# Folding the value and output weights, and moving the heads to partition quarters, in a Mamba and local-attention kernel

## The chip, the cores and the metric

The kernel runs on one core of one Trainium2 chip. The metric is device time in microseconds of one execution. The kernel before was run three times, and it has one profiled execution besides, taken by the hardware profiler. All times below are microseconds unless marked ns.

A core has five engines which run in parallel, each working through its own instructions in order: TensorE (PE, matrix products; its weight loads are shown apart as PEld), VectorE (DVE), ScalarE (ACT), GpSimd (POOL) and SyncE (SP). Here SyncE issues all DMA transfers of the kernel. Engines wait for each other through semaphores only.

## The reference, cut to what matters

The input x has 4 sequences of 1024 tokens with 128 features. First x gets a residual block: a layer norm, another, and two Mamba blocks (forward and backward scan over 1024 steps with 256 channels and 16 states). Then come six layers, each of them local attention and a feed-forward part, both with a residual:

```python
def attn_layer(x, Wqkv, qs, ksc, Wo):        # x: shifted tokens, 16 heads of 64
    q, k, v = split heads of (x @ Wqkv)
    q = l2norm(q) * qs;  k = l2norm(k) * ksc
    q = q * cos * scale + rotate_half(q) * sin * scale
    k = k * cos / scale + rotate_half(k) * sin / scale
    out = local_attention(q, k, v)            # windows of 32, each sees itself and the one before
    return out.reshape(b, n, INNER) @ Wo

def ffn_layer(x, g, bln, W1, b1, W2, b2):
    xn = (x - mu) / sqrt(var + 1e-05) * g + bln
    a, gate = split(xn @ W1 + b1, 2)          # 341 each
    return a * gelu(gate) @ W2 + b2
```

In local_attention the scores of a window of 32 queries against 64 keys are multiplied by 8, masked, put through a softmax, and multiplied with v. All is f32.

What the change rests on: for one head, attn @ (x Wv) @ Wo equals attn @ (x (Wv Wo)), since the product of a head's 128x64 value weights with its 64x128 output weights can be made ahead.

## The kernel before

The program has three parts. **Prepare** (class Prepare, L131 to L552) goes through eight units (four sequences, two directions): layer norms, input projections, convolution, the step sizes of the scan; what the scan needs is written to DRAM. On six of the units it also prepares one layer each: rotary tables times the q and k scales (lr, rm, rs), and the feed-forward weights scaled by the layer norm's gain (lf loads, fp and fv fold the bias, fa scales, fs stores). **Beside** (class Beside) does the scan: 512 steps of 128 rows (8 channels by 16 states) by 512 tokens, with one exponential on ScalarE (`decay`, L699), a product (`input`, L706 to L714), the scan on VectorE (`scan`, L731), a product on GpSimd (`output`, L744) and, for four steps, four column-quarter matmuls (`add`, L766). The first 134 steps lie in Prepare, the rest beside the layers. **Layers** (class Layers) does the six layers on tiles of 256 tokens, 96 tiles in all (four sequences, six layers, four tiles).

The order of the instructions is written out by hand in tables. ORDER has one entry for each operation with the number of tiles by which it lags: the row is run once a tile, so operations of five tiles are mixed. In ORDER six steps of Beside stand in each row (xd, xi, xr, xo, xt); once the scan is over, LAST_ORDER is used, which has none. FIRST_ORDER does the same for Prepare. All engines take their instructions in the order in which the tables issue them. Matmul results go to five PSUM banks that are handed out in turn (`one`).

One tile of Layers, operation by operation:

- `q` (L969 to L978): tokens are 128 rows, 512 columns of q or k weights are streamed; eight matmuls 128x512. `sq` (L981) squares on ScalarE, `rr` and `ro` (L994) multiply with the rotary tables on VectorE, `n` (L1002) sums squares, `ra` (L1007) adds the rotated halves on GpSimd, eight of 128x512, `nr` makes the inverse norms, `rs` (L1020) applies them.
- `v` (L1026) makes the values, four matmuls 128x512; `va` (L1032) copies them out; `vs` (L1042, L1043) makes a copy shifted by 32 rows by DMA, so that a window and the one before lie in one set of 64 rows.
- `t` and `qk` (L1057, L1067) transpose q and k on TensorE. `s`, `z` (L1078, L1096) write the mask and 128 small products into PSUM: query rows of a window in a quarter of the partitions (window number), head pairs and window halves along the columns. `mx`, `e`, `ex`, `sm`, `ew` (L1106 to L1127) are the softmax: maximum, subtraction (VectorE), one exponential of 128x1024 for eight heads (ScalarE), sum and reciprocal (VectorE), product (GpSimd).
- `te`, `at` (L1134, L1140) transpose the weights on TensorE and copy them out; `w`, `y` (L1159) multiply them with v, 128 matmuls of 64x64 by 32; `oe` (L1170) copies out, `pw` (L1181) multiplies with the output weights, eight matmuls of 128x256.
- `xf` to `xs` (L1199 to L1288): residual, norm, feed-forward part. `ge` adds the bias, `gelu` takes the table for Gelu in and the other back after it.

The weights of a layer are loaded for each sequence anew. `weight` counts the uses, and after the last one puts the next load on a list, `later`; the row's loop then issues one of the list at a time, on SP. Fetches of the scan's rows (`steps`, L671) go through SP as well.

## Time and profile before

| | |
|---|---|
| median of three runs | 4055.16 |
| lowest, highest | 4049.41, 4068.73 |
| span of the profiled execution | 4070.2 |
| mean granted TensorE clock | 0.959 |
| instructions | 145466 |
| HBM read, written | 381.42 MB, 51.67 MB |

The page shows nothing of the profiled execution outside its span, so the span stands for its own time; it is 15 us above the median of the runs.

How to read it: busy times are sums over one engine; a share near 100% says that the engine has hardly any idle time, not that each of its instructions is as short as it could be, since matmuls are pipelined and their ends are modelled. The groups' busy sums of TensorE overlap with one another, so what a group costs is better read from the chain of waits, or from the distance between starts in the timeline. The digits in the page's slices are tenths of a slice, of 101.8 us each.

### The profile page before, as it was taken

Reading aid. Unit: us, or ns where it says so; the run is one execution under the profiler, and the core shown is the slowest. Engines: PE = TensorE matmul, PEld = TensorE weight load, DVE = VectorE, ACT = ScalarE, POOL = GpSimd, SP = SyncE. Lnnn points to the kernel's source line nnn. Section 1 sums busy time; section 2 is a strip of 40 time slices with the busy share of each in tenths; the row PEclk is TensorE's granted clock in tenths of the full one; section 3 lists DMA queues with packets and bytes.
Section 4 is the critical chain, followed back from the end, with each engine's and each line's share of the span. In section 5 each row is a group of like instructions: output and inputs, shape, how many; then the busy total and the mean of one; then the engine's idle time right before and its main releaser. Section 6 shows DMA issues by size and latency. Waiting matters only on the chain.

```text
span 4070.2 us, 145466 instructions
## 1 busy us (share of the span) xinstructions
PE 3825.5 (94%) x62248; PEld 2447.0 (60%) x62248; DVE 3397.9 (83%) x5081; ACT 2975.5 (73%) x5581; POOL 3164.3 (78%) x2589
## 2 busy tenths in 40 slices
PE   5899859999999999999999999999999999999998
PEld 1333226666666666666666666666666666666665
DVE  3677769999899999999999999999777777777774
ACT  4577737887777787787777887877667777677775
POOL 2767669999889898998998998988666666566662
PEclk6788869999999999999999999999999999999999
DMA  5688855555545555555555555554221222122211
GB/s 156 190 268 267 250 178 149 148 161 154 149 133 159 145 154 153 161 151 148 154 145 142 156 156 158 153 151 118 58 65 54 64 58 74 52 63 57 66 50 40
DMA packets 319415, 540.05 MB, mean 133 GB/s; under 512 B 41795, under 2 KB 123467, under 8 KB 318771
## 3 DMA queue, kind: packets, MB, share of 16 engines
q1 hardware_dynamic: 318770, 530.75, 45.5%
q8 instruction: 492, 8.06, 0.9%
q14 instruction: 153, 1.25, 0.1%
HBM read 381.42 MB, written 51.67 MB: 106 GB/s over the span
## 4 chain that ended last, share of the span: by engine, by line
PE 70%; ACT 12%; DVE 7%; POOL 6%; issue 4%; DMA 1%; SPq 1%; DVEq 0%; ACTq 0%; POOLq 0%
PE pq L974 12%; PE po L1159 10%; PE pw L1181 8%; PE pv L1026 7%; PE pt L1057 6%; PE sim L1096 5%; PE pe L1134 4%; PE pm L290 3%; PE py L1278 3%; PE pa L1262 3%; PE pg L1238 2%; ACT sq L981 2%; PE acc L766 2%; DVE sh L731 1%; PE sim L1078 1%
## 5 line engine op out<-in xcount | busy, mean ns | idle before, releaser
L1007 POOL TENSOR_TENSOR r<-r,rot 128x512 f32<-128x512 f32 x768 | 964.1, 1274 | 83.2 <-DVE rot L994 71.1
L1020 POOL TENSOR_TENSOR r<-r,n 128x1024 f32<-128x1024 f32 x384 | 726.2, 1905 | 261.3 <-ACT n L1016 253.2
L974 PE MATMUL pq<-w,xsa 128*128 128x512 f32 x1536 | 799.0, 615 | 2.7 <-ACT at L1140 1.6
L744 POOL TENSOR_TENSOR sh<-sh,sc 128x512 f32<-128x512 f32 x512 | 649.9, 1274 | 96.9 <-DVE sh L731 66.7
L981 ACT ACTIVATE sq<-pq 128x512 f32<-128x512 f32 x768 | 448.2, 599 | 254.0 <-PE pq L974 125.4
L994 DVE TENSOR_TENSOR rot<-pq,tab 128x512 f32<-128x512 f32 x768 | 516.4, 683 | 133.9 <-ACT sq L981 111.0
L994 DVE TENSOR_TENSOR r<-pq,tab 128x512 f32<-128x512 f32 x768 | 518.1, 683 | 82.1 <-PE pq L974 40.3
L1127 POOL TENSOR_TENSOR e<-e,sm 128x1024 f32<-128x1024 f32 x192 | 365.5, 1904 | 243.6 <-DVE sm L1123 228.4
L1057 PEld LDWEIGHTS pt<-ident,r 128*128 128x128 f32 x3072 | 359.1, 142 | 242.5 <-issue 119.1
L1057 PE MATMUL pt<-ident,r 128*128 128x128 f32 x3072 | 443.4, 277 | 37.0 <-POOL r L1020 15.2
L1002 DVE TENSOR_REDUCE n<-sq 128x16 f32<-128x1024 f32 x384 | 456.6, 1210 | 0.0
L1159 PEld LDWEIGHTS po<-at,vs 64*64 64x64 f32 x12288 | 332.3, 135 | 198.3 <-issue 153.8
L1159 PE MATMUL po<-at,vs 64*64 64x32 f32 x12288 | 400.0, 223 | 21.5 <-issue 12.3
L1159 PE MATMUL po<-at,v 64*64 64x32 f32 x12288 | 391.6, 220 | 5.9 <-issue 5.8
L1026 PE MATMUL pv<-w,xsa 128*128 128x512 f32 x768 | 383.4, 601 | 0.2 <-ACT qT L1067 0.2
L1181 PE MATMUL pw<-o,wos 128*128 128x256 f32 x1536 | 377.9, 389 | 1.7 <-ACT o L1170 1.7
L731 DVE TENSOR_TENSOR_SCAN sh<-da,carry,sh 128x512 f32<-128x512 f32 x256 | 327.1, 1278 | 43.7 <-ACT da L699 41.2
L731 DVE TENSOR_TENSOR_SCAN sh<-da,sh 128x512 f32<-128x512 f32 x256 | 311.5, 1217 | 57.2 <-ACT da L699 50.6
L1096 PEld LDWEIGHTS sim<-kT,qT 64*32 64x32 f32 x24576 | 264.5, 106 | 141.8 <-issue 134.7
L1159 PEld LDWEIGHTS po<-at,v 64*64 64x64 f32 x12288 | 334.6, 136 | 9.0 <-issue 8.9
L699 ACT ACTIVATE da<-sdt,b_nega 128x512 f32<-128x512 f32 x378 | 260.5, 689 | 108.2 <-DVE sh L731 92.7
L974 PEld LDWEIGHTS pq<-w,xsa 128*128 128x128 f32 x1536 | 257.0, 191 | 125.8 <-issue 49.0
(160 smaller groups left out, 7598.5 us busy)
## 6 DMA issues: line engine op xcount, KB each, us to landing
sdt<-dts SPq DMA_DIRECT2D x756, 256.0 KB
vs<-v SPq DMA_DIRECT2D x192, 384.0 KB
fdt<-dts SPq DMA_DIRECT2D x204, 256.0 KB
w<-in_wqkv SPq DMA_DIRECT2D x288, 128.0 KB
tab<-tabs SPq DMA_DIRECT2D x96, 256.0 KB
vs<-v SPq DMA_DIRECT2D x168, 128.0 KB
wos<-in_wo SPq DMA_DIRECT2D x96, 128.0 KB
dts<-e SPq DMA_DIRECT2D x32, 256.0 KB
```

Source lines behind the costliest of these rows:

```text
L731: self.nc.vector.tensor_tensor_scan(h, self.da.pop(n), h, self.carry[:, at : at + 1] if t else 0.0, ALU.mult, ALU.add)
L744: self.nc.gpsimd.tensor_tensor(h, h, self.unit[k][2], ALU.mult)
L974: self.nc.tensor.matmul(pq, lhsT=self.tokens(t, i), rhs=w[:, g * 512 : (g + 1) * 512], start=True, stop=True)
L981: self.nc.scalar.activation(sq[:, g * 8 : g * 8 + 8], pq, AF.Square)
L994: self.nc.vector.tensor_tensor(out[:, g * 8 : g * 8 + 8], pq, tab, ALU.mult)
L1007: self.nc.gpsimd.tensor_tensor(r[:, :, to], r[:, :, to], rot[:, :, of], ALU.add)
L1020: self.nc.gpsimd.tensor_tensor(r, r, bc(n2[:, a, :], 2, [P, H, DH]), ALU.mult)
L1026: self.nc.tensor.matmul(pv, lhsT=self.tokens(t, i), rhs=w[:, g * 512 : (g + 1) * 512], start=True, stop=True)
L1057: self.nc.tensor.transpose(pt[:, j * P : (j + 1) * P], rf[:, (g * 4 + j) * P : (g * 4 + j + 1) * P], self.c["ident"],)
L1096: self.nc.tensor.matmul(t.bank["s", g, par][r * W : (r + 1) * W, col : col + 64], lhsT=qT[rows, g * 4 + j, at : at + W], rhs=kT[rows, g * ...
L1159: self.nc.tensor.matmul(t.bank["w", g, x][64 * par : 64 * par + 64, j * P + r * W : j * P + (r + 1) * W], lhsT=v[rows, col : col + DH], rh ...
L1181: self.nc.tensor.matmul(t.bank["pw"], lhsT=wos[:, g * 4 + h, :], rhs=t.tiles["o", g][:, h, :], start=(g == 0 and h == 0), stop=(g == 1 and ...
```

## The change

**The values.** Prepare gets operations that load a layer's value and output weights (wl), multiply them head by head (wp, 16 matmuls of a 64x128 by 64x128 pair), copy the products out (we) and store them (ws) as `wvo`, 16 matrices of 128x128. In Layers `v` now makes, for each window of 32 tokens, x Wv Wo of all heads: the heads are in four groups, and a group's results lie in a quarter of the partitions. `te`, `at`, `vs`, `y` and `pw` go.

**The heads on quarters.** `s` and `z` put head pair c of a half in quarter c of the partitions, and windows along the columns. The 32x32 blocks of the softmax weights are then transposed in place by VectorE (`tp`), and `w` sums over heads inside the matmul (128 rows are four heads by 32 keys): 64 matmuls of 128x32 by 128 a tile. `oe` copies 128x256, `ot` transposes it back.

**The softmax.** For one half of the heads (SINGLE) the maximum is negated, and the exponential is taken straight from PSUM, one of 64 columns for each head and window with the maximum as bias and the sum as a second output (`ea`), then `rc`; `e`, `ex`, `sm` stay for the other half.

**Smaller.** q's and k's columns are ordered so that a matmul holds one half of all heads; `rr`, `ro` and `sq` write with a stride, and `ra` becomes one addition of 128x1024 for each of four. The feed-forward weights are centred in Prepare (fc, fe), so `xn` reads xf and `xnc` goes. `ge` goes into `gelu` as a bias. `pg` and `pa` put two products in one bank. Weight loads stand in the tables (lw, lwv, l, ll, lt), with two buffers for wvo and lv and one for the others. xdbl and w1s in Prepare have one buffer instead of two. `decay`, `scan` and `output` get conditions on the others' progress. FIRST_ORDER, ORDER and LAST_ORDER are new.

The core of the diff, without the tables:

```diff
+    def fc(self, u, g):
+        if u.l is not None:
+            pm = u.bank["fc", g] = self.one("pm")[:, 0:FI]
+            self.nc.tensor.matmul(
+                pm, lhsT=self.c["center"], rhs=u.tiles["w1s", 0][:, g * FI : (g + 1) * FI],
+                start=True, stop=True,
+            )
+
+    def fe(self, u, g):
+        if u.l is not None:
+            self.nc.scalar.copy(
+                u.tiles["w1s", 0][:, g * FI : (g + 1) * FI], u.bank["fc", g]
+            )
...
+    def wl(self, u):
+        if u.l is not None:
+            for k, name in enumerate(("wvl", "wol")):
+                w = u.tile(self.sp, name, 0, [P, NHP, D])
+                self.nc.sync.dma_start(out=w, in_=self.values[k][u.l])
+
+    def wp(self, u, g, par):
+
+        if u.l is not None:
+            pm = u.bank["wp", g, par] = self.one("pm")
+            rows = slice(64 * par, 64 * par + 64)
+            for k in range(4):
+                self.nc.tensor.matmul(
+                    pm[:, k * D : (k + 1) * D], lhsT=u.tiles["wvl", 0][rows, g * 4 + k, :],
+                    rhs=u.tiles["wol", 0][rows, g * 4 + k, :], start=True, stop=True,
+                )
+
+    def we(self, u, g, par):
+        if u.l is not None:
+            self.nc.scalar.copy(
+                u.tiles["wol" if par else "wvl", 0][:, g * 4 : g * 4 + 4],
+                u.bank["wp", g, par].rearrange("p (k m) -> p k m", m=D),
+            )
+
+    def ws(self, u, par):
+        if u.l is not None:
+            of = u.tiles["wol" if par else "wvl", 0]
+            for g in range(2):
+                self.nc.sync.dma_start(
+                    out=self.values[2][u.l, :, :, 2 * g + par, :], in_=of[:, g * 4 : g * 4 + 4]
+                )
...
+    def load(self, name, l, *of):
+        tile_ = partial(self.wp.tile, dtype=F32, name=name, bufs=1 + (name in TWICE))
+        if name[:2] == "qk":
+            w = tile_([P, 512])
+            at = int(name[2]) * H * DH + int(name[3]) * 512
+            pairs = [(w, wqkv[l, :, at : at + 512])]
+        elif name == "wvo":
+            w = tile_([P, 4, 4 * D])
+                (w[:, c].rearrange("p (n m) -> p n m", m=D), wvo[l, :, c]) for c in range(4)
...
+    def begin(self, t, name):
+        if t.sb == 0 and t.k:
+            self.load(name, t.l)
+
+    def lw(self, t, a, g):
+        self.begin(t, f"qk{a}{g}")
...
-    def ra(self, t, i, a, x):
-        r, rot = t.tiles["r", (i, a)], t.tiles["rot", (i, a)]
-        to, of = slice(x * W, x * W + W), slice(W - x * W, 2 * W - x * W)
-        self.nc.gpsimd.tensor_tensor(r[:, :, to], r[:, :, to], rot[:, :, of], ALU.add)
+        self.nc.vector.tensor_reduce(
+            n2[:, a, :], t.tiles["sq", (i, a)].rearrange("p h x e -> p h (x e)"), AX.X, ALU.add
+        )
+
+    def ra(self, t, i, a):
+        r = t.tiles["r", (i, a)].rearrange("p h x e -> p (h x e)")
+        rot = t.tiles["rot", (i, a)].rearrange("p h x e -> p (h x e)")
...
-    def v(self, t, i, g):
-
-        w = self.weight("w2", t)
-        pv = t.bank["v", i, g] = self.one("pv")
-        self.nc.tensor.matmul(
-            pv, lhsT=self.tokens(t, i), rhs=w[:, g * 512 : (g + 1) * 512], start=True, stop=True
-        )
-
-    def va(self, t, i, g):
-        v = t.tile(self.sp, "v", i, [P, H * DH], 4)
-        self.nc.scalar.copy(v[:, g * 512 : (g + 1) * 512], t.bank["v", i, g])
-
-    def vs(self, t, i):
-
-        nc, v = self.nc, t.tiles["v", i]
-        vs = t.tile(self.sp, "vs", i, [P, H * DH], 4)
-        if t.sb == 0 and i == 0:
-            nc.gpsimd.memset(vs[0:W], 0.0)
-        else:
-            before = t.tiles["v", 0] if i else self.tile_at(t, -1).tiles["v", 1]
-            nc.sync.dma_start(out=vs[0:W], in_=before[P - W : P])
-        nc.sync.dma_start(out=vs[W:P], in_=v[0 : P - W])
+    def v(self, t, w):
+
+        wvo = self.weight("wvo", t)
+        pv = t.bank["v", w] = self.one("pv")
+        at = W + t.sb * SB + w * W
+        for c in range(4):
+            self.nc.tensor.matmul(
+                pv[c * W : (c + 1) * W], lhsT=self.xsa[t.b % 2][:, at : at + W], rhs=wvo[:, c],
+                start=True, stop=True,
+            )
+
+    def va(self, t, w):
+        vw = t.tile(self.sp, "vw", w, [P, 4, D], VALUES)
+        self.nc.scalar.copy(vw, t.bank["v", w].rearrange("p (n m) -> p n m", m=D))
...
+    def products(self, t, g, windows):
         qT, kT = t.tiles["qT", 0], self.kT
-        for j in js:
-            for x in range(2):
-                for r in range(4):
-                    at = P * (r // 2) + 64 * x + W * (r % 2)
-                    for par in range(2):
-                        rows = slice(64 * par, 64 * par + 64)
-                        col = (j * 2 + x) * 64
-                        self.nc.tensor.matmul(
-                            t.bank["s", g, par][r * W : (r + 1) * W, col : col + 64],
-                            lhsT=qT[rows, g * 4 + j, at : at + W],
-                            rhs=kT[rows, g * 4 + j, at : at + 2 * W],
-                            start=False, stop=(j == 3 and x == 1),
-                        )
+        for w in windows:
+            for c in range(4):
+                for par in range(2):
+                    rows = slice(64 * par, 64 * par + 64)
+                    self.nc.tensor.matmul(
+                        t.bank["s", g, par][c * W : (c + 1) * W, w * 64 : (w + 1) * 64],
+                        lhsT=qT[rows, g * 4 + c, w * W : (w + 1) * W],
+                        rhs=kT[rows, g * 4 + c, w * W : (w + 2) * W],
+                        start=False, stop=(w == 7),
+                    )
...
+        self.nc.vector.tensor_reduce(
+            mx[:, par * 8 : par * 8 + 8], sv, AX.X, ALU.max, negate=g in SINGLE
+        )
+
+    def ea(self, t, g, par):
+
+        e = t.tile(self.sp, "e", g, [P, 16, 2 * W], 2)
+        sm = t.tile(self.sp, "sm", g, [P, 16], 2)
+        mx = t.tiles["mx", g]
+        sv = t.bank["s", g, par].rearrange("p (n j) -> p n j", j=2 * W)
+        for w in range(8):
+            n = par * 8 + w
+            self.nc.scalar.activation(
+                e[:, n], sv[:, w], AF.Exp, bias=mx[:, n : n + 1], accum_out=sm[:, n : n + 1]
+            )
+
+    def rc(self, t, g):
+        sm = t.tiles["sm", g]
+        self.nc.vector.reciprocal(sm, sm)
...
-    def te(self, t, g, par):
-
-        ef = t.tiles["e", g].rearrange("p (h x) j -> p h (x j)", x=2)
-        pe = t.bank["te", g, par] = self.one("pe")
-        for j in range(4):
...
+    def tp(self, t, g):
+
+        eT = t.tile(self.sp, "eT", g, [P, 2, 8, 2, W], 2)
+        self.nc.vector.transpose(
+            eT.rearrange("p a w x q -> p (a w x q)"),
+            t.tiles["e", g].rearrange("p n j -> p (n j)"),
+        )
+
+    def w(self, t, g, i):
+
+        if g == 0 and i == 0:
+            t.bank["o"] = self.one("po")[:, 0:SB]
+        t.weighted += 1
+        eT = t.tiles["eT", g]
+        before = None if t.sb == 0 else self.tile_at(t, -1)
+        begun = set()
+        for par in range(2):
+            for x in range(2):
+                for r in range(4):
+                    at = 4 * i + r - 1 + x
+                    of = t if at >= 0 else before
+                    if of is None:
+                        continue
+                    first = g == 0 and i == 0 and r not in begun
+                    begun.add(r)
+                    self.nc.tensor.matmul(
+                        t.bank["o"][r * W : (r + 1) * W, i * D : (i + 1) * D],
+                        lhsT=eT[:, par, 4 * i + r, x, :],
+                        rhs=of.tiles["vw", at % 8][:, 2 * g + par, :],
+                        start=first, stop=(t.weighted == 4 and par == 1 and x == 1),
+                    )
+
+    def oe(self, t):
+        self.nc.scalar.copy(t.tile(self.sp, "o", 0, [P, SB], 2), t.bank["o"])
+
+    def ot(self, t):
+
+        pw = t.bank["pw"] = self.one("pw")[:, 0:SB]
+        for i in range(2):
             self.nc.tensor.transpose(
...
-    def pw(self, t, g):
...
-    def xnc(self, t):
-        self.nc.scalar.copy(t.tile(self.sp, "xn", 0, [P, SB]), t.bank["pd"])
...
     def xn(self, t):
-        xn = t.tiles["xn", 0]
-        self.nc.vector.tensor_tensor(xn, t.bank["pvar"], xn, ALU.mult)
+        self.nc.vector.tensor_tensor(
+            t.tile(self.sp, "xn", 0, [P, SB]), t.bank["pvar"], t.tiles["xf", 0][:, 0:SB], ALU.mult
+        )
...
     def scan(self):
+        if self.at["scan"] == min(self.at["decay"], self.at["input"]):
+            return
...
+SINGLE = (1,)
...
+TWICE = "wvo", "lv"
```

Of the new tables, the part of ORDER that holds `w` and what follows it:

```text
ro100-1 rr100-1 sq100-1 xo-0 xr-0 s1-2 ra10-1 z1-2 rr111-1 l1-3 sq111-1 lw11-0 v6-3 mx10-2 xt-0
w00-3 lw10-0 xq-0 va6-3 xa-0 rs00-1 w01-3 ro111-1 xd-0 lt-0 mx11-2 w10-3 xo-0 w11-3 lw00-0 xi-0
xp-0 py0-4 sm0-2 ea10-2 xp-0 n10-1 oe-3 py1-4 ot-3 xq-0 xq-0 py2-4 v2-2 n11-1 t001-1 ea11-2 ll-3
xf-3 ew0-2 xo-0 va2-2 nr1-1 xi-0 t000-1 xs-4 xr-0 qk001-1 t011-1 qk000-1 t010-1 xq-0 q011-0
qk010-1 qk011-1 sq011-0 rs10-1 rc1-2 tp0-2 xp-0 lw01-0 q001-0 pd-3 xd-0 xt-0 rr011-0 xq-0 xt-0
```

## The prediction

> **What bounds the kernel now.** I read the page first, then the busy time of the engines in two stretches, then the chain of waits of the second stretch, then stretches of the timeline. The page's span is 4070.2 us. TensorE is nearly full from slice 6 on; VectorE and GpSimd are nearly full only in slices 6 to 27.
>
> ```profile
> span 4070.2 us, 145466 instructions
> PE 3825.5 (94%) x62248; PEld 2447.0 (60%) x62248; DVE 3397.9 (83%) x5081; ACT 2975.5 (73%) x5581; POOL 3164.3 (78%) x2589
> PE   5899859999999999999999999999999999999998
> DVE  3677769999899999999999999999777777777774
> POOL 2767669999889898998998998988666666566662
> PEclk6788869999999999999999999999999999999999
> ```
>
> So there are three stages: *prepare* (0 to about 600 us), the *main loop* (600 to about 2830, Layers and Beside together, table ORDER) and the *last loop* (to the end, Layers alone, LAST_ORDER). Next come the two loops by engine. The columns are the stretch, its length, busy time of PE, PEld, DVE, ACT and POOL, clock, DMA share and GB/s.
>
> ```profile
> 700.00:2800.00 2100.00, 2041.20 (x36450) 1366.84 (x36450) 1975.32 (x2873) 1628.52 (x3105) 1917.30 (x1574) 1.00 0.54 151
> 2900.00:3900.00 1000.00, 983.08 (x18179) 680.98 (x18178) 756.25 (x1171) 725.16 (x1396) 630.57 (x448) 1.00 0.21 60
> ```
>
> VectorE's subtractions `e` (four a tile, below) number 227 and 116 there, so the stretches hold 56.75 and 29.0 tiles. One tile takes 37.0 us in the main loop (PE 36.0, DVE 34.8, POOL 33.8, ACT 28.7) and 34.5 us in the last (PE 33.9, DVE 26.1, ACT 25.0, POOL 21.7). TensorE bounds both, at 97 and 98%; in the main loop VectorE stands 6% behind it. From 600 to 2830 there are 60 tiles' time, from 2830 to 4070 36.
>
> The chain of waits for 2900 to 3900 us shares that time out by line, free of the overlap that the groups' busy sums contain:
>
> ```profile
> by line: PE pq L974 21.1%; PE po L1159 12.5%; PE pw L1181 11.1%; PE pv L1026 10.4%; PE pt L1057 9.8%; PE sim L1096 8.5%; PE pe L1134 5.4%; PE pg L1238 4.1%; PE py L1278 3.8%; PE pa L1262 3.7%; PE sim L1078 2.4%; PE pd L1207 1.3%; PE pvar L1
> ```
>
> Of 34.5 us a tile: po 4.31, pw 3.83, pv 3.59, pe 1.86.
>
> **The change, TensorE.** These four go: -13.6 us a tile. In their place come 32 matmuls of 128x512 in column quarters for v, 64 of 128x128 in quarters for w, and 2 transposes. Nothing in the old layers has that form, but Beside's add does: four quarters of 128x512, each in two passes. The timeline (start, length, engine, line, what, count; a start minus the one before is what the step really costs):
>
> ```profile
> 1511.05 1.06 PE L766 MATMUL acc<-sh,wide 128*32 128x512 f32 x8
> 1512.05 0.66 PE L1057 MATMUL pt<-ident,r 128*128 128x128 f32 x4
> ...
> 3318.66 1.02 PE L974 MATMUL pq<-w,xsa 128*128 128x512 f32 x2
> 3319.52 1.02 PE L1026 MATMUL pv<-w,xsa 128*128 128x512 f32 x2
> 3320.37 1.02 PE L974 MATMUL pq<-w,xsa 128*128 128x512 f32 x2
> ...
> 3330.80 1.13 PE L974 MATMUL pq<-w,xsa 128*128 128x512 f32 x2
> 3331.86 0.32 PE L1159 MATMUL po<-at,vs 64*64 64x32 f32 x8
> ```
>
> Four quarters take 1.00 us, one full matmul 0.86; so quarters do run side by side. A full one between two other array shapes takes 1.06: a change of shape costs about 0.1. For v, 8 windows give 6.9 us without any change of shape and 8.0 at the add's price; the tables put v in about five groups, so 6.9 + 5 x 0.14 = 7.6. For w, 16 groups of four quarters, each a quarter of the 512 columns, 0.215 us: 3.4, with entries 3.7. The upper end for w is that its 128 weight loads don't hide: L1159's loads show 332.3 us for 12288, 27 ns each, +3.5 us; I take the low end since add's loads (128x32 as well) hide. The transposes cost 2 x 0.11 (four `pt` in 0.44). Sum +11.5: net **-2.0 us a tile** (-3.0 to +1.5). TensorE: 31.9 in the last loop, 34.0 in the main loop.
>
> **VectorE.** Out: two subtracts `e` (0.60 each from start to start) and one sum `sm` (1.21); in: two 32x32 transposes of 128x1024. The rotary products, `n`, `mx` keep their sizes, only with runs of 32 elements; `xn` too. No transpose is in the trace. Its nearest rows are passes over the same 1024 elements:
>
> ```profile
> L1112 DVE TENSOR_TENSOR e<-sim,mx 128x512 f32<-128x512 f32 x227 | 145.5, 684 | 0.0
> L1122 DVE TENSOR_REDUCE sm<-e 128x16 f32<-128x1024 f32 x114 | 138.2, 1212 | 1.8
> ```
>
> From 1.21 (one pass) to 2.42 (two) each; I take 1.21, as every f32 row of 1024 on VectorE stands near it. Sum -2.4 + 2.4: VectorE stays at 34.8 and 26.1. The Trainium skill (VectorE: DVE Perf Modes, The three transpose paths) gives 311 ns for a 128x128 bf16 transpose; as an estimate, eight of these are 2.49 us, which is the bad end, and no run here shows one yet.
>
> **ScalarE.** `at` (4) goes and `va` doubles (+4): equal. `oe` 4x512 becomes 1x256: -1.7. One `ex` of 1024: -0.97. `xnc` -0.28, `ge` 3 x 0.40 = -1.2, gelu three instead of two +0.3. In come 16 exponentials of 64 elements with a bias column and a running sum. The nearest row, `n` 128x32 with a bias column, has 0.32; 32 more elements at (0.597 - 0.372)/256 us make 0.35. Back-to-back copies overlap by 0.1 (two in 1.07 against 0.587 each), so 0.25 is the low end; no overlap and one more instruction for the sum, priced at the shortest row (0.188, L1194), is the high end, 0.54. I take 0.375: +6.0 (4.0 to 8.6). Net +2.2: 27.2 and 30.9 us, at worst 29.8 and 33.5, still under TensorE and VectorE. The rule that speaks against this part is in the Trainium skill (ScalarE: Activation LUTs, What ACT_TABLE_LOAD costs): about 280 ns fixed with a bias column plus 0.833 ns an element, an estimate of 333 ns here and 5.3 us for 16; by it ScalarE would be 0.7 us lower.
>
> **GpSimd.** `ra` 8 x 1.274 (L1007) becomes 4 of 1024 elements; the row with two full inputs (x1b, L245) has 2.354: -0.8, so 33.0 and 20.9. Not a bound.
>
> **SyncE and DMA.** The 360 shifted copies of v go, with SP's waits ahead of them (225 us in the main loop, 773 in the last, at L1043). The weights' bytes for a layer are the same 2 MB plus FFN. A load now stands at a fixed place behind its last reader; it waits at SP's head, and fetches of sdt are queued behind it. The reader of qk01 is issued some 70 entries ahead of the load, so I price this at nothing; if the cover fails, one 256 KB load late by about 3 us on every fourth tile is 24 x 3 = 72 us.
>
> **Prepare.** Six units gain 16 matmuls of 64x128 by 128 (4 x 0.215 x 4 = 3.4 us on TensorE), two of 128x341 (1.1), six copies on ScalarE (4 x 0.5 + 2 x 0.45 = 2.9), and 2 MB of DMA (wl, ws), 12 MB against 131 MB up to 600 us. From 200 to 500 us PE is 91% busy at clock 0.83 and DMA 84%. w1s, wvl and wol have one buffer, so each next load waits on SP until the store has landed, with the fetches of dt behind it; they run five steps ahead. 4.5/0.83 x 6 = 33 us if TensorE's part shows in full; below, nothing; above, with DMA (12 MB at 260 GB/s = 46 us) some 70. I take **+30**.
>
> **Sum.** Last loop: 31.9/0.983 = 32.5, -2.0 x 36 = -72 us. Main loop: VectorE, 34.8, is late next, with TensorE 34.0 and GpSimd 33.0 close behind. VectorE's idle there is 6%, most of it released by PE; at 97% a tile takes 35.9, -1.1 x 60 = -66. The new conditions on decay, scan and output let all six steps of a row pass except two outputs of the first, so the scan ends at most one row later (35.9 - 32.5 = 3 us, within the rounding). Prepare +30. Together -108: 3962 for the profiled execution. Its span is 15 us over the median of the runs (4055.2; nothing outside the span is shown), so **3947** on the median, -2.7%.
>
> **Rivals.**
> - *More*: v at 6.9 with few shape changes, VectorE at 98.5% in the main loop, prepare hidden: -3.0 x 36 - 1.65 x 60 = -207, 3848. For it: the new tables have 11 and 13 shape changes in TensorE's order where the old had 14 and 18. Against: four engines within a few per cent seldom leave only 1.5% idle.
> - *Main loop gains nothing*: 37.0 stays, since VectorE, GpSimd, five PSUM banks and ScalarE's queue (eight exponentials in a row hold two banks and keep `sq` and `qk` behind them) give back what TensorE is spared; prepare +50: -72 + 50 = -22, 4033.
> - *Slower*: the transpose takes two passes, 2.42. Main loop: VectorE 34.8 + 2.4 = 37.2, at 97% 38.4, +84 us; the last loop keeps its -72 (VectorE 28.5 is under 31.9); prepare +30: +42, 4097. It decides from 2.1 us a transpose on ((72 - 30)/60 = 0.7 us a tile). Speaks for it: no such row in the trace; against: no f32 row of 1024 is above 1.3.
> - *The packing fails* for w (weight loads show, net +1.5): +54 + 90 + 30, over 4200. Add's row speaks against it.
>
> **Chances.** Forecast 0.45; more 0.20; main loop without gain 0.17; slower by the transpose 0.13; packing 0.05. Within 0.5% is about what a measurement can't tell from no change: 4035 to 4075. Half of the third case lies under it: faster 0.45 + 0.20 + 0.07 = 0.72, same 0.11, slower 0.17. The range runs from just under *more* to the transpose case, 3830 to 4095.
>
> **What would show it.** Transposes at 1.2 us; 8 quarter matmuls of v in 1.0 us or less from start to start; exponentials at 0.25 to 0.54; the last loop near 32.5 us a tile with PE still at 98%; the main loop near 35.9 with DVE at 97%; the layers starting some 30 us later. It is wrong if TensorE gets idle in the last loop (ScalarE's queue or the banks then set the pace) or if SP's loads appear as releasers of `pq`.

## The result and the profile after

The changed kernel takes **4105.6 us** (median of four runs, 4100.2 to 4106.1) beside 4053.8 for the kernel before on the same chip: 1.0113 times as long, 95% interval 1.0088 to 1.0137. The forecast was 3947, faster. The profiled execution's span is 4103.3 us, 33 more than before.

The page after, the lines that answer to those of before:

```profile
PE 3708.1 (90%) x52480; PEld 2014.2 (49%) x52480; DVE 3369.7 (82%) x4985; ACT 3080.1 (75%) x8017; POOL 3089.0 (75%) x2181
PE   5889858999899899999899999999999999999998
DVE  4666668999899999999999999899877777777775
```

TensorE was spared 117 us of busy time, and the span grew all the same: its nines of the main loop have become a mix of eights and nines. The busy time of the engines in the two stretches used before (columns as there) says it in numbers:

```profile
700.00:2800.00 2100.00, 1932.42 (x30175) 1082.54 (x30172) 1943.40 (x2782) 1664.30 (x4465) 1853.27 (x1320) 1.00 0.41 122
2900.00:3900.00 1000.00, 954.48 (x15411) 551.95 (x15410) 753.88 (x1166) 760.74 (x2141) 623.59 (x335) 0.99 0.10 31
```

TensorE fell from 97 to 92% in the main loop and from 98 to 95% in the last. No engine took its place: VectorE stands at 92.5%, GpSimd at 88%.

Where the time went is read from the starts of one instruction, `xf` of VectorE, once a tile ("row"). The table gives the start of the first `pq`, of `xf` of the tiles 5 and 55, and the mean distance of two rows in the main loop (tiles 5 to 55) and in the last (65 to 85), worked out from the traces:

| kernel | first pq | tile 5 | tile 55 | row, main | row, last |
|---|---|---|---|---|---|
| before | 555.0 | 825.1 | 2676.3 | 37.02 | 34.21 |
| after | 578.6 | 871.4 | 2743.1 | 37.43 | 33.59 |
| forecast | +30 | | | 35.9 | 32.5 |

Up to tile 5 the change loses 46 us, in the main loop 0.4 a row instead of winning 1.1, and in the last loop it wins 0.6 a row instead of 2.0.

What the profile offers as a reason: the squares of q and k (`sq`, ScalarE), one line of the groups of before and one of after. The two numbers behind the bar are the time idle ahead of them and the part of it that the releaser named ended.

```profile
L981 ACT ACTIVATE sq<-pq 128x512 f32<-128x512 f32 x768 | 448.2, 599 | 254.0 <-PE pq L974 125.4
```

```profile
L1042 ACT ACTIVATE sq<-pq 128x512 f32<-128x512 f32 x768 | 460.2, 600 | 458.9 <-DVE rot L1055 218.2
```

The squares and the two rotary products `r` and `rot` (VectorE) read the same PSUM bank, and the program makes its readers wait for one another by semaphores: one engine at a time. Before, TensorE ended about half of the squares' waiting (125.4 of 254.0 us); now VectorE ends nearly all of it (218.2 us with `rot` and 209.5 with `r`, of 458.9). ScalarE's waits from 700 to 2700 us, before and then after (total us, times, longest):

```profile
ACT sq L981 <- DVE r L994: 74.7, 103, 1.7
...
ACT sq L981 <- PE pq L974: 30.4, 76, 0.8
...
ACT sq L981 <- DVE rot L994: 10.8, 11, 1.5
```

```profile
ACT sq L1042 <- DVE r L1055: 174.2, 107, 2.7
ACT sq L1042 <- DVE rot L1055: 78.9, 95, 1.6
```

86 us of waiting for VectorE's products became 253, and VectorE's own waits for squares went from 11 to 88 us (51.8 ahead of `r`, 35.8 ahead of `rot`). The waiting reaches TensorE through the banks: `pa` uses nothing that `rot` makes, only a bank that `rot` has to leave first, and this is now TensorE's longest wait from 700 to 2700 us, 42.6 of 160 us idle; before, it didn't occur:

```profile
PE pa L1317 <- DVE rot L1055: 42.6, 47, 1.8
```

In the timeline of the last loop the two engines hand two banks to and fro. ScalarE and then VectorE, after:

```profile
3330.03 0.60 ACT L1042 ACTIVATE sq<-pq 128x512 f32<-128x512 f32 x1 [1.11 <-DVE rot L1055]
...
3331.98 0.60 ACT L1042 ACTIVATE sq<-pq 128x512 f32<-128x512 f32 x1 [0.57 <-DVE rot L1055]
3332.48 1.05 ACT L1186 ACTIVATE e<-e 128x1024 f32<-128x1024 f32 x1
3334.33 0.31 ACT L1168 ACTIVATE e<-sim,mx 128x64 f32<-128x64 f32 x1 [0.80 <-DVE mx L1156]
...
3338.48 1.28 ACT L1308 ACT_TABLE_LOAD   x1
```

```profile
3329.32 0.68 DVE L1055 TENSOR_TENSOR rot<-pq,tab 128x512 f32<-128x512 f32 x1
3330.66 0.69 DVE L1055 TENSOR_TENSOR r<-pq,tab 128x512 f32<-128x512 f32 x1 [0.66 <-ACT sq L1042]
3331.27 0.68 DVE L1055 TENSOR_TENSOR rot<-pq,tab 128x512 f32<-128x512 f32 x1
3332.61 0.69 DVE L1055 TENSOR_TENSOR r<-pq,tab 128x512 f32<-128x512 f32 x1 [0.66 <-ACT sq L1042]
3333.22 0.41 DVE L1283 TENSOR_TENSOR xn<-pvar,xf 128x256 f32<-128x256 f32 x1
3333.55 0.68 DVE L1156 TENSOR_REDUCE mx<-sim 128x8 f32<-128x512 f32 x1
```

`rot` ends at 3330.0, only then the square runs, only then `r` of the same bank; `rot` of the next bank follows, and so again. Behind them come the maximum, the block of eight exponentials (3334.33 to 3336.8), and the table for Gelu at 3338.48.

The Trainium skill (PSUM — Partial Sum Buffer, PSUM bank collisions raise a hardware error) says that ScalarE and VectorE may not access the same bank and the same 32 partitions at once, two reads included. In the trace none of the 768 squares overlaps a product of its bank, which is in line with it; what such a collision would do, no run here shows.

### The profile page after: what moved, and what is told of

It reads as the page before. It is cut to its first block, busy times and chain, and to the rows that moved or that the text cites. A ratio compares the mean times of both kernels' runs of the same rounds, so it can differ in the third digit from the quotient of the medians.

```text
span 4103.3 us, 126265 instructions
## 1 busy us (share of the span) xinstructions
PE 3708.1 (90%) x52480; PEld 2014.2 (49%) x52480; DVE 3369.7 (82%) x4985; ACT 3080.1 (75%) x8017; POOL 3089.0 (75%) x2181
## 5 line engine op out<-in xcount | busy, mean ns | idle before, releaser
L1067 POOL TENSOR_TENSOR r<-r,rot 128x1024 f32<-128x1024 f32 x384 | 910.1, 2374 | 264.6 <-DVE rot L1055 249.4
L1042 ACT ACTIVATE sq<-pq 128x512 f32<-128x512 f32 x768 | 460.2, 600 | 458.9 <-DVE rot L1055 218.2
L1035 PE MATMUL pq<-qk,xsa 128*128 128x512 f32 x1536 | 776.2, 609 | 17.2 <-DVE rot L1055 9.4
L1089 PE MATMUL pv<-wvo,xsa 128*32 128x512 f32 x6144 | 756.6, 601 | 28.6 <-ACT ge L1308 15.3
L1195 POOL TENSOR_TENSOR e<-e,sm 128x1024 f32<-128x1024 f32 x192 | 365.4, 1903 | 218.2 <-DVE sm L1174 206.4
L1096 ACT COPY vw<-pv 128x512 f32<-128x512 f32 x768 | 441.5, 587 | 61.2 <-PE pv L1089 53.3
L1168 ACT ACTIVATE e<-sim,mx 128x64 f32<-128x64 f32 x1536 | 457.8, 334 | 24.6 <-DVE mx L1156 22.8
L1222 PE MATMUL po<-vw,eT 128*32 128x128 f32 x12096 | 415.9, 279 | 47.7 <-issue 41.6
L1222 PEld LDWEIGHTS po<-vw,eT 128*32 128x32 f32 x12096 | 368.3, 112 | 139.5 <-issue 87.9
L1035 PEld LDWEIGHTS pq<-qk,xsa 128*128 128x128 f32 x1536 | 261.0, 191 | 279.7 <-issue 82.9
L1089 PEld LDWEIGHTS pv<-wvo,xsa 128*32 128x32 f32 x6144 | 158.9, 109 | 416.4 <-issue 165.7
L1168 ACT ACTIVATION_READ_ACCUMULATOR e<-sim,mx 128x1 f32 x1536 | 349.5, 228 | 0.0
```

The source lines that it names most:

```text
L1035: self.nc.tensor.matmul(pq, lhsT=self.tokens(t, i), rhs=w, start=True, stop=True)
L1042: self.nc.scalar.activation(sq[:, :, g], pq, AF.Square)
L1067: self.nc.gpsimd.tensor_tensor(r, r, rot, ALU.add)
L1089: self.nc.tensor.matmul(pv[c * W : (c + 1) * W], lhsT=self.xsa[t.b % 2][:, at : at + W], rhs=wvo[:, c], start=True, stop=True,)
L1168: self.nc.scalar.activation(e[:, n], sv[:, w], AF.Exp, bias=mx[:, n : n + 1], accum_out=sm[:, n : n + 1])
L1222: self.nc.tensor.matmul(t.bank["o"][r * W : (r + 1) * W, i * D : (i + 1) * D], lhsT=eT[:, par, 4 * i + r, x, :], rhs=of.tiles["vw", at % 8 ...
```

## The experiments

Ratios are to the kernel before, run on the same chip in the same minutes. A ratio of 1.0113 is "no different from the change as it stands". Rows are those of the table above; busy times of a row are taken over the same rows. In the diffs, a line of table entries lists those that are moved or left out, without the rest of their rows, and where an edit has further lines the text says what they do.

**1. Without the folding in Prepare.** The raw weights are loaded as wvo; wl, wp, we and ws are left out, so the values aren't folded.

```diff
-                (w[:, c].rearrange("p (n m) -> p n m", m=D), wvo[l, :, c]) for c in range(4)
+                (w[:, c].rearrange("p (n m) -> p n m", m=D), wvo[c // 2][l, :, c % 2 * 4 : c % 2 * 4 + 4])
+                for c in range(4)
...
-wl-0 wp00-1 wp01-1 we00-1 we01-1 wp10-1 wp11-1 we10-1 we11-1 ws0-1 ws1-1
```

> The changed kernel without the fold in Prepare: wl, wp, we and ws are left out, and the layers load the raw value and output weights (the same bytes) in place of the products, so the output is not the reference's. Theory 1 (the fold's own matmuls, copies and 2 MB of transfers a layer are what Prepare lost): the first q comes some 20 us earlier (578.6 now), the first rows of the layers some 40 us, and the time falls from 4105 to about 4065. Rival (the new order of Prepare, the single buffers and fc/fe are the cause): the time falls by at most 10 us.

Measured 4065.6, ratio 0.9989 (0.9977 to 1.0001): 1.24% under the change, 50 us. The first `pq` starts at 544.2, rows 37.20 and 33.71. So the folding costs 50 us, and without it the change is as fast as the kernel before, no faster: the loops, as they stand, win nothing. Of the 50 us, 36 show up to tile 5 (835.1 in place of 871.4) and some 12 in the 50 rows of the main loop.

**2. Its traffic alone.** wp and we are left out; loads, stores and the layers' loads stay (values not folded).

```diff
-wp00-1 wp01-1 we00-1 we01-1 wp10-1 wp11-1 we10-1 we11-1
```

> Leaves out the folding's transposes and products with their copies (wp, we), and keeps its loads of the raw weights, its stores and the loads that the layers make of what was stored (the values stored are not folded). Leaving out all of the folding gave back 50 us of the changed kernel's time. Theory TRAFFIC (the loads and stores of the folding, one buffer each, and SyncE standing in front of them with the fetches of Beside behind it are the cost): the time stays within 12 us of the changed kernel, 4094 or more, and the first pq starts at 575 us or later. Theory WORK (its matmuls and copies on the full TensorE and ScalarE of Prepare are the cost, 40 us by the count of the prediction): 4070 or less, the first pq near 550. In between, the share of each is read off directly.

4069.3, ratio 1.0017 (1.0004 to 1.0030), first `pq` at 553.5. Of the folding's 50 us the traffic is 0.28%, 11 us (give or take 7, by the two intervals), and the products and copies 0.96%, 39 us: mostly WORK, as the prediction had it, only more of it.

**3. Short exponentials for all heads.**

```diff
-SINGLE = (1,)
+SINGLE = (0, 1)
...
-e00 e01 ex0 sm0
+ea00 ea01 rc0
```

> The changed kernel with the short exponentials for all heads (e, ex and sm of the first half replaced by ea and rc at e's places). VectorE loses two subtractions and one sum, 2.4 us a row, ScalarE gains about 3.7. Theory A (the main loop's row is VectorE's busy time plus about 2.7 us of waits): rows of the main loop fall from 37.4 to some 35.5, limited then by GpSimd and ScalarE at 33 each; time about 4000, below the kernel before. Theory B (blocks of exponentials in ScalarE's queue hold everything else up): rows get longer by 1 us or more, time 4150 or more. Theory C (a loop of waits in the table that no engine's busy time sets): within 20 us of 4105.

4443.2, ratio 1.0917 (1.0887 to 1.0946); rows 40.60 and 37.98, though no engine is busy for more than 35.3 us of a row. Sparing VectorE 2.1 us a row and loading ScalarE by 3.7 costs 3.2 and 4.4 us. Part of it may be the clock: the granted clock was 0.97 and 0.96 in the two stretches of rows, beside 0.995 in the change, and TensorE's busy time is 0.8 and 1.7 us a row longer.

**4. A quarter of the transpose.** Only 256 of 1024 columns are transposed (the softmax weights used are those of a quarter).

```diff
-            t.tiles["e", g].rearrange("p n j -> p (n j)"),
+            t.tiles["e", g].rearrange("p n j -> p (n j)")[:, 0:256],
...
```

> The changed kernel with VectorE transposing only a quarter of the softmax weights (256 of 1024 columns; w reads that quarter for all windows, so the output is not the reference's). VectorE loses about 1.8 us a row, nothing else changes. Theory A (VectorE sets the main loop): -1.5 to -1.8 us a row of the main loop, nothing in the last, time about 4000 to 4015. Theory C (a loop of waits): 0 to -20 us.

4082.6, ratio 1.0034 (1.0019 to 1.0049); main row 36.99. VectorE was spared 1.5 us a row and the row fell by 0.44: VectorE alone doesn't set the main loop.

**5. Half of `w`.** Only the odd head of each pair is multiplied, half of the matmuls of `w`.

```diff
-        for par in range(2):
+        for par in (1,):
```

> The changed kernel with half of the matmuls of w (only odd heads are summed, so the output is not the reference's). TensorE loses about 1.9 us a row. Theory A (VectorE sets the main loop, TensorE the last): main loop as before, last loop 33.6 to 31.9 us a row, time about 4045. If TensorE still sets both: about -170 us, 3935. If a loop of waits sets the last loop as well: within 20 us of 4105.

4061.6, ratio 0.9987 (0.9973 to 1.0000). Main row 36.58 (-0.85), last row 33.92 (+0.33); none of the three forms had that. In the last loop, where TensorE was thought to set the pace, 1 us less of it brings nothing, so TensorE's busy time alone doesn't set that loop any more. The granted clock was 0.97 there beside 0.995 in the change, so part of what was spared may have gone into slower matmuls. In the main loop 1.5 us less of TensorE brings 0.85: there it is still part of what holds the row.

**6. No short exponentials.** `e`, `ex`, `sm` for both halves, all else as changed.

```diff
-SINGLE = (1,)
+SINGLE = ()
...
-ea10-2 ea11-2 rc1-2
+e10-2 e11-2 ex1-2 sm1-2
```

> The second half of the heads goes back to one subtraction of the maximum on VectorE, one exponential of 1024 and one sum, at the places in the tables where the short exponentials stood; all else of the change stays. Per row ScalarE loses 4.7 - 1.1 = 3.6 us, VectorE gains 1.2 + 1.2 = 2.4 us (34.7 to 37.1 in the main loop, 27.6 to 30.0 in the last). Theory BLOCK (the block of eight exponentials lies on the chain that times a row of the last loop, 2.3 us between the maximum and the FFN's table load): the subtraction (0.6) and the long exponential (1.0) take 1.6 in its place, so the last loop falls by about 0.7 us a row, to 32.9, 25 us in all; the main loop becomes VectorE's, 37.1 busy and 38.4 a row, +60: together about 4140. Rival THE BLOCK IS HIDDEN (TensorE or the rotary chain times the rows): the last loop stays at 33.6 or rises, and the main loop rises as before.

4188.4, ratio 1.0316 (1.0301 to 1.0331). Main row 38.59 with VectorE busy for 36.9, as expected; the last row rose to 34.06 where BLOCK had 32.9. The block isn't dearer than what stands in its place here. In the timeline of this run two sums of squares `n` lie on VectorE between the maximum (3306.18) and its subtraction (3309.03); that this is why the row rose isn't shown.

**7. The kernel before with the short exponentials.**

```diff
-e10-2 e11-2 ex1-2 sm1-2
+ea10-2 ea11-2 rc1-2
```

> The kernel before, with the short exponentials alone: for half the heads two blocks of eight exponentials with a bias column and a running sum in place of two subtractions, one long exponential and one sum. TensorE's work stays, 36.0 and 33.9 us a row. VectorE loses 2.4 us a row, ScalarE gains 3.6 (28.7 to 32.3 and 25.0 to 28.6). Theory BLOCK (a block of exponentials lies on the chain of a row when nothing else is spared): the last loop rises by about 1 us a row (34.2 to 35), the main loop by 0 to 1 us: 4085 to 4150. Rival BUSY SUMS (TensorE times the rows, ScalarE has 4 us to spare): the last loop stays at 34.2, the main loop at 37.0 or a little less: 4040 to 4075.

4269.3, ratio 1.0509 (1.0488 to 1.0529). Last row 35.13, as BLOCK had it; main row 39.40, far above its 37 to 38. Alone, this part costs 5%, with all engines' work of a row under 37 us.

**8. Blocks of four instead of eight.** Exponentials of 128 columns, two windows with the maximum of the first and one sum, so that the softmax isn't the reference's; `rc` and `ew` are fitted to the four sums.

```diff
-        for w in range(8):
+        for w in range(0, 8, 2):
             n = par * 8 + w
             self.nc.scalar.activation(
-                e[:, n], sv[:, w], AF.Exp, bias=mx[:, n : n + 1], accum_out=sm[:, n : n + 1]
+                e[:, n : n + 2], sv[:, w : w + 2], AF.Exp, bias=mx[:, n : n + 1],
+                accum_out=sm[:, n : n + 1],
             )
...
```

> Four exponentials of 128 columns in place of eight of 64 in each block; the bias and the sum of a pair are those of its first head, so the softmax is not that of the reference, and every other instruction stays in number (the last multiplication is given the sums of pairs). A block shrinks from 2.33 us to 4 x 0.34 = 1.4 by (0.597 - 0.372)/256 us for each more column, so ScalarE is spared 1.9 us a row. Theory BLOCK (the blocks hold the rows): the last loop falls by about 0.9 us a row, since one block is on its chain, to 32.7, and the main loop by 0.5 to 1.5, to 36.3: 4015 to 4060. Rival (ScalarE is no part of what times a row): both loops within 0.2 us of the changed kernel, 4095 to 4110.

4088.7, ratio 1.0065 (1.0043 to 1.0087). Last row 32.69 (-0.90, as BLOCK had it), main row 37.61 (+0.2, as its rival had it), and the time lies between the two. The block of 2.3 us lies on the chain of the last loop; in the main loop it isn't what holds the row.

**9. Softmax without a maximum, in the changed kernel.**

```diff
-        self.nc.vector.tensor_tensor(
-            e[:, s], sv, bc(t.tiles["mx", g][:, s], 2, [P, 8, 2 * W]), ALU.subtract
-        )
+        self.nc.scalar.activation(e[:, par * 8 : par * 8 + 8], sv, AF.Exp)
...
-mx00 mx01 mx10 mx11 ex0 ea10 ea11 rc1
+e10 e11 sm1
```

> The changed kernel with a softmax without the maximum, for all heads: four exponentials of 128x512 straight from the PSUM banks, no maximum and no subtraction, one sum of 128x1024 for each half of the heads (q and k have unit length and a scale of 8, so exp can't overflow and the quotient is the same). Per row VectorE loses 4 x 0.68 + 2 x 0.6 - 1.2 = 2.7 us (34.7 to 32.0 in the main loop, 27.6 to 24.9 in the last) and ScalarE 5.7 - 2.4 = 3.3 us; TensorE's 34.5 and 32.1 stay. Theory CHAIN (the time that TensorE was spared is lost in the steps of ScalarE and VectorE between its matmuls, the block of exponentials and the maximum ahead of it among them): the last loop falls by 1 us or more a row, to 32.6 or less, which is then TensorE's 32.1 at 98%; the main loop falls by 1 to 2 us, to 35.4 to 36.4; in all 3960 to 4020, below the kernel before. Rival (something else that the new tables fixed, such as the banks or GpSimd, times the rows): less than 0.4 us a row in either loop, 4080 or more.

4064.2, ratio 1.0010 (1.0001 to 1.0019). Last row 32.38 as CHAIN had it, main row 37.30: taking 2.3 us of VectorE and 3.6 of ScalarE out of a main row leaves it where it was. ScalarE's squares still wait 232 us for products there.

**10. The same softmax in the kernel before.**

```diff
-mx00 mx01 mx10 mx11 ex0 ex1
```

> The same softmax without a maximum in the kernel before: VectorE loses 4 x 0.68 + 4 x 0.6 = 5.1 us a row (34.9 to 29.8, 26.1 to 21.0), ScalarE gains 4 x 0.6 - 2 x 1.05 = 0.3, TensorE's 36.0 and 33.7 stay. Theory: TensorE times the rows of the kernel before, so the last loop stays within 0.3 us of 34.2 and the main loop falls by no more than 0.7 us, to 36.3 or above: 4010 to 4062. If the folded kernel with the same softmax is below this one, the folding pays as soon as TensorE sets the pace again; if it is above, the folding's 50 us in Prepare outweigh what TensorE is spared. Rival (VectorE times the main loop of before, TensorE only stands full beside it): main loop to 35.5 or less, 3970 or less.

4069.6, ratio 1.0016 (1.0005 to 1.0028); rows 36.98 and 33.55. VectorE's main row is 4.7 us shorter and the row is unmoved: TensorE sets it in the kernel before. The last row fell by 0.7, more than expected, the time as a whole didn't. And the folded kernel with the same softmax only draws level.

**11. Squares that don't read the bank.**

```diff
-        pq = t.bank["q", i, a, g].rearrange("p (h e) -> p h e", e=W)
-        self.nc.scalar.activation(sq[:, :, g], pq, AF.Square)
+        tab = t.tab.rearrange("p n k e -> p (n k e)").rearrange("p (h e) -> p h e", e=W)
+        self.nc.scalar.activation(sq[:, :, g], tab, AF.Square, scale=1e-14)
```

> ScalarE's squares read the rotary table in SBUF (128x512, the same size) in place of the bank with q or k, so ScalarE and VectorE no longer take turns at that bank; the norms, and so the softmax, are not the reference's, and every instruction stays in number. In the changed kernel ScalarE waits 257 us in the main loop's 2000 us ahead of these squares (4.8 us a row) and VectorE 90 us. Theory TURNS (taking turns at the bank with q is what the new tables made worse: the waits of squares for VectorE grew from 86 us to 253): the main loop falls by 1 us or more a row, to 36.4 or less, and the last by 0.5 or more, to 33.1: 4030 or less. Rival (these waits are idle time of a ScalarE that has nothing else to do yet): both loops within 0.4 us: 4080 to 4110.

**3933.5, ratio 0.9689** (0.9672 to 0.9705): 172 us under the change. Rows 35.04 and 32.76. The two stretches, the second 900 us long here:

```profile
700.00:2800.00 2100.00, 2022.34 (x32279) 1150.69 (x32272) 2038.53 (x2959) 1788.30 (x4770) 1969.80 (x1392) 1.00 0.43 127
2900.00:3800.00 900.00, 864.55 (x14308) 508.35 (x14301) 691.88 (x1070) 705.90 (x1982) 574.42 (x308) 1.00 0.10 32
```

VectorE is at 97% in the main loop, TensorE at 96% in both: near what the forecast had said of the changed kernel. ScalarE's and VectorE's waits for one another at these banks are gone, and TensorE's 42.6 us of `pa` waiting for `rot` are 0.2.

**12. Half of GpSimd's rotary sum.** Half of q and k lacks the rotated part.

```diff
-        self.nc.gpsimd.tensor_tensor(r, r, rot, ALU.add)
+        self.nc.gpsimd.tensor_tensor(r[:, 0:512], r[:, 0:512], rot[:, 0:512], ALU.add)
```

> GpSimd adds the two rotary products for half of the columns only (4 x 128x512 in place of 4 x 128x1024 a row; the other half of q and k lacks the rotated part). GpSimd is spared 4 x 1.2 = 4.7 us a row: 33.9 to 29.2 in the main loop, 23.3 to 18.6 in the last. Theory GPSIMD (its 33.9 us of 37.4, with VectorE's products released late, time the main loop): the main loop falls by 1 us or more a row, 4045 or less, and the last loop stays. Rival (GpSimd is late because its inputs are): main loop within 0.4 us, 4080 to 4110.

4095.9, ratio 1.0089 (1.0074 to 1.0104), main row 37.29 with GpSimd 4.3 us shorter: not GpSimd.

**13. Squares off the bank in the kernel before** (norms not the reference's).

```diff
...
-        self.nc.scalar.activation(sq[:, g * 8 : g * 8 + 8], pq, AF.Square)
+        self.nc.scalar.activation(sq[:, g * 8 : g * 8 + 8], tab, AF.Square, scale=1e-14)
```

> The kernel before with its squares reading the rotary table in place of the bank (as in the run with the changed kernel, which that made 172 us shorter). Theory TURNS, in its strong form (the kernel before hardly pays for turns, the changed one does): the time falls by 50 us at most, 4010 or more, main loop 36.3 or above. Weak form (both kernels pay about alike, and the changed one lost its gain elsewhere): it falls by 100 us or more, 3960 or less. The difference between this run and the changed kernel without turns is what the change is worth when the bank's turns cost nothing in either.

4060.6, ratio 1.0005 (0.9994 to 1.0017), rows 36.71 and 33.98. The strong form holds: the turns cost the kernel before nothing that can be measured. Its TensorE is busy for 97 and 99% of the stretches here, and hides them.

**14. Turns put into the kernel before.** Five squares are moved between the products of their bank.

```diff
 rr010-1
+sq010-1
 ro010-1
-sq010-1
```

> The kernel before with five entries moved so that squares stand between the two products of their bank in 5 of 8 banks of ORDER (1 of 8 before) and 2 of 8 of LAST_ORDER (1 of 8). Nothing else changes. Theory BETWEEN: the main loop rises by 0.7 to 1.5 us a row, to about 38, the last by 0.1 at most, 4095 to 4150. Rival (the place of the square doesn't matter): within 0.3 us a row, 4045 to 4080.

4197.8, ratio 1.0342 (1.0319 to 1.0364). Main row 39.01 (+2.0, more than expected), last row 34.17. The same instructions in the same number; what is added is waiting. ScalarE's and then VectorE's waits, 700 to 2700 us:

```profile
ACT sq L981 <- DVE r L994: 89.5, 78, 2.6
...
ACT sq L981 <- DVE rot L994: 76.8, 50, 2.3
```

```profile
DVE r L994 <- ACT sq L981: 79.4, 113, 1.3
DVE rot L994 <- ACT sq L981: 75.4, 99, 1.4
```

ScalarE 166 us in place of 86, VectorE 155 in place of 11. The places of five squares in the order, alone, are worth 3.4%.

**15. Turns mended in the changed kernel.** Six squares (4 of 8 banks in ORDER, 2 of 8 in LAST_ORDER) are moved from between the products to just ahead or behind.

```diff
-rr010-1 s0-2 sq010-1 ro010-1
+rr010-1 s0-2 ro010-1 sq010-1
```

> The changed kernel with six entries of the tables moved: wherever a square stood between the two rotary products of the same bank (4 of 8 banks in ORDER, 2 of 8 in LAST_ORDER), it stands ahead of both or behind both. No instruction more or less, and nothing moves by more than 15 entries. Theory BETWEEN (a square between the two products hands the bank from VectorE to ScalarE and back, so both queues wait for one another twice; the kernel before has 1 of 8 in each table): the main loop falls by 1 us a row or more, to 36.4 or below, the last by some 0.3, 4020 to 4045, and the waits of squares for VectorE fall by half. Rival (any shared reading of the bank costs it, wherever the square stands): less than 0.4 us a row, 4080 or more.

4117.1, ratio 1.0143 (1.0120 to 1.0165): no gain, as its rival had it. BETWEEN as the whole explanation falls. ScalarE waits 229 us for `rot` where it waited 253 for both: a square close behind a product waits just as one between two.

**16. Run 15 with the softmax without a maximum** (the edits of runs 9 and 15 together).

> The changed kernel with the six moved entries and with the softmax without a maximum. Theory: the two ease different steps, the turns in the main loop and the maximum with the block of exponentials in the last; the last loop comes to 32.3 as with the softmax alone, the main loop to 36.0 or less, 3970 to 4010, below both kernels. Rival (the moved entries do nothing): 4060, as with the softmax alone.

4097.3, ratio 1.0094 (1.0071 to 1.0118), rows 37.97 and 32.37. The last loop is as in run 9; the moved entries cost 0.7 us a row in the main loop.

**17. Squares ahead by six entries**, ten entries moved.

```diff
-ro101-1 va1-3 rs01-1 sq101-1 xd-0 ro100-1 rr100-1 sq100-1
+sq100-1 ro101-1 va1-3 rs01-1 xd-0 ro100-1 sq111-1 rr100-1
```

> The changed kernel with its squares moved ahead of both rotary products of their bank, by six entries where there is room (ten entries of the tables moved in all, nothing added). Moving six of them to just ahead or just behind gave nothing, and ScalarE then waited for the products 229 us in place of 253. Theory LATE SQUARES (in the new tables the squares stand near or behind the products, VectorE is behind the table, so ScalarE's queue stops at them; ahead by some entries they find the bank free): ScalarE's waits for the products fall below 80 us in 700 to 2700, the main loop falls by 1 us a row or more toward the 35.0 that it has without turns, the last toward 32.8: 3950 to 4040, below the kernel before. Rival (VectorE then waits for the squares instead, since ScalarE is no less behind): VectorE's waits for squares rise above 150 us in the same stretch, and the time stays at 4090 or more.

4116.5, ratio 1.0140 (1.0124 to 1.0157). ScalarE's waits for the products are gone from the list of 700 to 2700 us; these stand there instead, ScalarE's and VectorE's:

```profile
ACT sq L1042 <- PE pq L1035: 77.5, 92, 1.7
```

```profile
DVE r L1055 <- ACT sq L1042: 66.6, 88, 1.7
DVE rot L1055 <- ACT sq L1042: 30.3, 59, 0.9
```

Neither form was right. ScalarE's waits for the products went, but 77.5 us for `pq` stand in their place and the time didn't fall; VectorE's waits rose only from 88 to 97. The main row fell by 0.4 (37.00) and the last rose by 1.1 (34.72), where ScalarE now waits 98 us for TensorE's `pq`.

**18. Run 17 with the softmax without a maximum** (the edits of runs 9 and 17 together).

> The same with the softmax without a maximum, which spares ScalarE 3.3 us and VectorE 2.7 us a row and took 1.2 us from the last loop. If the squares no longer stop ScalarE, the main loop has 32.0 us of VectorE, 26 of ScalarE, 34 of TensorE and GpSimd and comes to 34.8 to 36, the last to 32.3: 3920 to 4010. If the rival of the run beside it holds, about 4060, as with this softmax alone.

4063.0, ratio 1.0009 (0.9999 to 1.0018), rows 36.15 and 34.86. In the main loop the lead is worth 1.15 us a row once ScalarE is eased (run 9: 37.30); in the last it costs 2.5. Run 17's ORDER with the old LAST_ORDER and this softmax wasn't tried. No version that leaves nothing out was faster than the kernel before.

## Why the prediction was wrong

**The step that failed is the sum**: "VectorE, 34.8, is late next ... at 97% a tile takes 35.9", and TensorE at 98.3% of a last row. Both take the busy sums for the bound and leave out that ScalarE and VectorE take turns at the banks of q and k. The trace of before showed this, 86 us of `sq` waiting for `r` and `rot` in 2000, in a kernel where it cost nothing. With TensorE spared and the new tables it costs 172 us (run 11 against the change), in the kernel before none (run 13). With the turns out of both kernels the change is 3933.5 - 4060.6 = **-127 us**; the forecast had -108. So about the gain that it summed up is there once the turns are gone, though not split as foreseen: more of it comes in the main loop and less in the last.

| term | forecast | as measured | with squares off the bank in both (runs 11, 13) |
|---|---|---|---|
| up to tile 5 | +30 | +46 | +31 |
| main loop, a row | -1.1 | +0.4 | -1.7 |
| last loop, a row | -2.0 | -0.6 | -1.2 |

Point by point:

- *TensorE, -2.0 a row*: near. Busy time fell by 1.6 us, from 33.7 to 32.1 a last row, and by 1.5 a main row; with squares off the bank in both (runs 11, 13) it is 2.1 and 1.9. The timeline of the last loop has six windows of `v` in a row, each four quarters in two passes:

```profile
3320.96 5.36 PE L1089 MATMUL pv<-wvo,xsa 128*32 128x512 f32 x48
3326.25 1.13 PE L1035 MATMUL pq<-qk,xsa 128*128 128x512 f32 x2
```

  5.29 us from start to start, 0.88 a window. Summed from start to start a row has 7.5 of `pv` and 4.7 of `po` (4.1 without waits); foreseen were 7.6 and 3.7.
- *VectorE, transpose at 1.21*: right. The line of the last loop's groups:

```profile
L1200 DVE STREAM_TRANSPOSE eT<-e 128x1024 f32<-128x1024 f32 x59 | 72.7, 1232 | 0.3
```

  The bad end that was worked out from a page of the Trainium skill (VectorE: DVE Perf Modes, The three transpose paths), 2.49 us, is refuted by this row. The rival *slower by the transpose* fell with it.
- *ScalarE, exponentials at 0.375*: the size was on the high side. Two instructions each, which overlap:

```profile
L1168 ACT ACTIVATE e<-sim,mx 128x64 f32<-128x64 f32 x464 | 138.3, 333 | 20.2 <-DVE mx L1156 18.6 <-POOL kT L1103 1.6
L1168 ACT ACTIVATION_READ_ACCUMULATOR e<-sim,mx 128x1 f32 x464 | 105.0, 226 | 0.0
```

  From start to start one takes 0.29 us, a block 2.3. What was missed is that a block is a wait, not a load: in the last loop it lies between the maximum and the table for Gelu; run 8 wins 0.9 us a row by shortening it, run 9 1.2 by leaving it out together with the maximum. Turns (run 11, -0.8) and block seem to stand in one chain there: without either the row comes to within 0.3 us of the 32.5 of the forecast.
- *Prepare, +30*: the net was near, +24 at the first `pq` and +31 at tile 5 with squares off the bank in both, but by luck: the parts were not as foreseen. Folding is 50 us (run 1), 39 of them work and 11 traffic. It puts the first `pq` back by 34 (578.6 - 544.2), and the rest of the change brings it forward by 11 (555.0 - 544.2), which the prediction didn't have.
- *SyncE's loads at nothing*: right. Loads release 0.9 us of `pq`'s waiting from 700 to 2700, and from 2900 to 4000 `pq` waits 0.1 us in all.
- *Rivals*: by its number *slower by the transpose* (4097) came nearest, which is luck, since its transpose is refuted. By its mechanism "main loop gains nothing" (4033) did. It named ScalarE's queue, with the exponentials holding `sq`; for the main loop runs 8 and 9 speak against the exponentials, and run 11 for the turns of `sq`.

**What stays open.** Run 11 takes away three things at once: the turn, the square's hold on the bank, and the square's wait for `pq`. They weren't told apart. TensorE's waits for banks that `rot` holds, 42.6 us in the change and 0.2 in run 11, show only that banks held longer are part of it. Nor was an order found that removes the turns: moved close (15) or ahead (17), the wait turns up at the other engine, at TensorE or in the other loop. That the new tables are the cause, and not the operations, is shown in part only: run 14 shows that an order can cost this much with the old operations; that some order with the new ones doesn't is not shown.

## What to carry to other kernels

Ahead of the sum by busy times, list the buffers that two in-order engines share, and read the waits between them in the trace of before: a wait that costs nothing under a full engine can become the bound when that engine is relieved. A freed engine is worth its time only if the chain of the others, handovers included, fits in what remains; leaving out one reader of a shared bank is a cheap run that shows this bound. And a part's worth on its own (short exponentials, +5% in the kernel before) says little of its worth beside the others.

## What the runs showed of the hardware

- An exponential with a running sum of 64 columns is an ACTIVATE of 0.33 us and a read of the accumulator of 0.23 us, 0.29 us from start to start; of 128 columns 0.37 and 0.21.
- VectorE's 32x32 transpose of 128x1024 f32 takes 1.23 us, as much as a sum over the same elements.
- Column-quarter matmuls of 512 columns run at 0.88 us for four when six sets of four stand in a row, about one full matmul's 0.86.
